# First attention of a two-layer decoder: row maxima and the stack of queries in chunks of 256 instead of 512

## The chip, the cores and the metric

The kernel runs on one core of one Trainium2 chip. TensorE (PE) multiplies matrices into PSUM banks, VectorE (DVE), ScalarE (ACT) and GpSimd (POOL) work beside it, and SyncE (SP) issues the DMAs. Each engine takes its own instructions strictly in the order in which the program gives them; semaphores order the engines among each other. The metric is the time of one execution on the device in microseconds (us). Before the change it was 2409.12 us, the median of 3 runs from 2406.58 to 2414.77 us.

## The reference, cut to what matters

Two decoder layers work on x of shape (4, 1024, 256). Each layer has a self-attention, a cross-attention to a short context, and a feed-forward part, all with a layer norm ahead and a residual behind. The change is in the first self-attention: 16 heads of 16 elements, causal, with a linear bias by distance (ALiBi).

```python
qkv = x @ w_attn.T                                   # x: 4 batches, 1024 tokens
att = jnp.einsum('bhqd,bhkd->bhqk', q, k) * (1.0 / math.sqrt(D))
bias = jnp.where(causal, slopes * rel, -jnp.inf)     # rel = key position - query position
att = jax.nn.softmax(att + bias[None], axis=-1)
y = jnp.einsum('bhqk,bhkd->bhqd', att, v)
```

The second layer's self-attention squares its scores instead of exponentiating them and has gates in place of the bias; the change touches it only in how queries are laid out.

## The kernel before

**Stages.** The first half of the execution does the first attention (`A0`) of batch 0, 1, 2, 3 in turn. Woven into batch b's attention are the cross-attention and feed-forward of batch b-1 and the preparation of weights. The second half does the same with the second attention (`A1`), from about 1274 us on, and ends with the last feed-forward.

**Groups and stacks.** `A0` takes the 16 heads in four groups of 4, so there are 16 groups over the four batches. For a group, `stacks` (L310) loads two tiles from DRAM on SP's queue. `QS` holds queries, `KS` keys, with 96 rows of split-up query and key parts (bf16, three parts each, in two sets of 48 rows), 12 rows for the bias, and two rows (108 and 109) for the negated row maximum of every query, split into a high and a low bf16 part. The product of a KS block with a QS block over all 110 rows is then the finished exponent: score plus bias minus row maximum. QS has shape [110, 2, 4, 512]: two halves of 512 queries, in each 4 heads. Its 96 rows are loaded with four DMAs (two sets of rows by two halves, L323), KS with two (L320), and one DMA each brings the bias rows (L325, L326). QS and KS have two buffers each. `A1` uses the same `stacks` for its 20 loads, without the bias rows.

**Row maxima.** `a0_max` (L339) goes through the scores once to find the maxima. One unit multiplies QS blocks of 128 queries with up to 512 keys into one PSUM bank (L352), adds the causal mask with a further matmul where the block lies on the diagonal (L356), and reduces with DVE (L357). The banks are named M and there are two (2 and 3), shared with the projections of queries, keys and values, named Q. A group has 38 units: 11 for the diagonal parts of queries 0 to 511, 11 for those of queries 512 to 1023, and 16 for the latter against keys 0 to 511. Then L372 joins the two sets of maxima of the second half.

**Putting them.** `a0_put_max` (L375) is called twice per group, after unit 11 and after unit 38. DVE negates 16 columns (L380), PE transposes them into an M bank (L381), ACT copies the high part (L383), DVE subtracts to get the low part (L384), and two DMAs on SP's queue write the rows 108 and 109 of one half of QS (L386).

**The main pass.** `a0_main` (L388) goes through the queries in four chunks c of 256 and through the key blocks j up to the diagonal: 2, 4, 6 and 8 units, 20 per group. A unit has four score matmuls (L401), with the mask (L403) where needed, two exponentials on ACT (L404), and, two units later, four products with the values (L413) into the one O bank. Chunks 0 and 1 read the first half of QS, chunks 2 and 3 the second.

**What sets the order.** `A0` (L470) weaves the main pass of group g with the loads and row maxima of group g+1, 20 main units to 25 or 38 units of the other side; in each batch the third group's side also holds the first 12 steps of the next batch's projections, and the fourth group's side the rest with the row maxima of that batch's first group. `schedule` weaves this with the side work. The result is only a priority. The framework then plans each engine's order with a time model of its own and takes later work ahead where it believes that earlier work is not ready. So the main pass of group g+1 begins in the measured order while the last maxima of group g+1 are still being made. That order is fixed when the program is built; it doesn't adapt on the chip.

Of the kernel before, what the change touches and what calls it, by code (L numbers as in the profile page):

```python
# [12 lines left out]
F32 = mybir.dt.float32  # L13
# [17 lines left out]
def const_arrays():  # L31
    bf = ml_dtypes.bfloat16
    c = {}
# [48 lines left out]
    c["alq"] = np.ascontiguousarray(rq.reshape(4, 4, 12, 2, 512).transpose(2, 0, 3, 1, 4)).astype(bf)  # L82
# [8 lines left out]
class Kern:  # L91
# [218 lines left out]
    def stacks(self, g, dr, alibi):  # L310

        nc = self.nc
        QS = self.t([110, 2, 4, 512], BF, "QS")
        KS = self.t([110, 4, T], BF, "KS")
        c, o = g // 2, (g % 2) * 4
        for st, t0 in ((QS, (1, 0)), (KS, (4, 5))):
            for r in range(2):
                v = dr[c][t0[r] : t0[r] + 3].rearrange("t (d h) n -> (t d) h n", h=8)[:, o : o + 4, :]
                if st is KS:
                    nc.sync.dma_start(KS[r * 48 : r * 48 + 48], v)  # L320
                else:
                    for a in range(2):
                        nc.sync.dma_start(QS[r * 48 : r * 48 + 48, a], v[:, :, a * 512 : a * 512 + 512])  # L323
# [15 lines left out]
    def a0_max(self, st, mt, tag="M"):  # L339
# [4 lines left out]
        def unit(pieces, diag, out):  # L344
# [6 lines left out]
            for x, (hh, i, k0, k1) in enumerate(pieces):  # L351
                nc.tensor.matmul(Sv[:, x, 0:w], QS[:108, i // 4, hh, i % 4 * 128 : i % 4 * 128 + 128], KS[:108, hh, k0:k1], start=x == 0, stop=not diag and x == n - 1)  # L352
# [6 lines left out]
        for part in range(2):  # L359
            b0 = part * 4  # L360
            yield unit([(hh, b0, part * 512, part * 512 + 128) for hh in range(4)], True, mt[:, :, b0])
            for p in range(2):
                yield unit([(p * 2 + e, b0 + 1, part * 512, part * 512 + 256) for e in range(2)], True, mt[:, p * 2 : p * 2 + 2, b0 + 1])
            for i in (2, 3):
                for hh in range(4):
                    yield unit([(hh, b0 + i, part * 512, part * 512 + (i + 1) * 128)], True, mt[:, hh, b0 + i : b0 + i + 1])
            if part == 0:
                self.a0_put_max(st, mt, 0)
        for i in range(4, 8):
            for hh in range(4):  # L370
                yield unit([(hh, i, 0, 512)], False, mt[:, hh, 4 + i : 5 + i])
        nc.vector.tensor_tensor(mt[:, :, 4:8], mt[:, :, 4:8], mt[:, :, 8:12], ALU.max)  # L372
        self.a0_put_max(st, mt, 1)

    def a0_put_max(self, st, mt, part):  # L375

        nc = self.nc
        ps = self.p("M")
        m8 = self.t([128, 4, 4], F32, "_m8")
        nc.vector.tensor_scalar(m8, mt[:, :, part * 4 : part * 4 + 4], -1.0, None, ALU.mult)  # L380
        nc.tensor.transpose(ps[:16, :128], m8.rearrange("p h i -> p (h i)"), self.ident)  # L381
        pr = self.t([16, 2, 128], BF, "VsJ")
        nc.scalar.activation(pr[:, 0, :], ps[:16, :128], AF.Copy)  # L383
        nc.vector.tensor_tensor(pr[:, 1, :], ps[:16, :128], pr[:, 0, :], ALU.subtract)  # L384
        for p in range(2):
            nc.sync.dma_start(st[0][108 + p : 109 + p, part].rearrange("o h (i n) -> o (h i) n", n=128), pr[:, p, :])  # L386

    def a0_main(self, st, V, y, g, O, pend):  # L388
# [3 lines left out]
        def scores(c, j):  # L392
# [4 lines left out]
            for p in range(2):  # L397
                S = self.p("S").rearrange("p (h k) -> p h k", h=2)
                for e in range(2):
                    hh = 2 * p + e  # L400
                    nc.tensor.matmul(S[:, e, 0:w], st[1][:110, hh, j * 128 : (j + 1) * 128], st[0][:110, q0 // 512, hh, q0 % 512 : q0 % 512 + w], start=e == 0, stop=not dg and e == 1)  # L401
# [421 lines left out]
    def A1(self, parts):  # L823
# [50 lines left out]
        def scores(r, b, g, c, j):  # L874
# [19 lines left out]
            for p in range(2):  # L894
                S = self.p("S").rearrange("p (h k) -> p h k", h=2)
                for e in range(2):
                    hh = 2 * p + e
                    nc.tensor.matmul(S[:, e, 0:w], st[r][1][:96, hh, j * 128 : (j + 1) * 128], st[r][0][:96, q0 // 512, hh, q0 % 512 : q0 % 512 + w], start=e == 0, stop=e == 1)  # L898
# [427 lines left out]
```

## Time and profile before

| What | Value |
|---|---|
| Median of 3 runs | 2409.12 us |
| The profiled execution | 2408.58 us |
| its span, from first to last instruction | 2406.8 us |
| PE busy | 2141.5 us (89%) |
| DVE busy | 1692.2 us (70%) |
| ACT busy | 1639.2 us (68%) |
| POOL busy | 1198.2 us (50%) |
| Reduces of the row maxima, L357 | 608, 386.2 us on DVE |
| Score matmuls for the maxima, L352 | 768, 225.8 us on PE |
| DMA | 238.45 MB, mean 99 GB/s |

The span is the time between the first and the last recorded instruction on the core; the execution's own time has 1.8 us around it. A busy time is the union of an engine's instructions. A row of the form "x608 | 386.2, 655 | 137.9 <-PE M L356 100.0" says: 608 instructions, 386.2 us busy together, 655 ns mean, 137.9 us in which the engine stood idle just before one of them, 100.0 us of that ended by the PE instruction of line 356. "PEclk" is the TensorE clock granted, as a share of full speed. L and a number is a line of the kernel before.

### The profile page before, as it was taken

To read this page: it belongs to the slowest core of one execution; us is meant where nothing else is said; L and a number is where in the kernel's file an instruction comes from. 1 tells how busy PE (TensorE), PEld (TensorE's weight loads), DVE (VectorE), ACT (ScalarE), POOL (GpSimd) and SP (SyncE) were. 2 spreads that over 40 slices of the span, in tenths; PEclk is the share of its full clock that TensorE was granted. 3 is DMA by queue.
4 is the path that set the end of the run, shared out by engine and by line. 5 is a ranking of instruction groups with operands and counts; after the bars stand their busy time and mean duration, and the time that the engine had idled before them with its cause. 6 is when DMAs were issued, how large, how long until landed. Compare 5 with 4: busy or idle time off the path is not lost.

```text
span 2406.8 us, 51445 instructions
## 1 busy us (share of the span) xinstructions
PE 2141.5 (89%) x19110; PEld 1510.9 (63%) x19110; DVE 1692.2 (70%) x3781; ACT 1639.2 (68%) x4173; POOL 1198.2 (50%) x1942
## 2 busy tenths in 40 slices
PE   6798899998999998899988988889988998899876
PEld 4454457755666654576656766567766766676675
DVE  4666657677766786776775677777867787777766
ACT  4365446676766676565778878987678777888542
POOL 7121313154331352412545458766867788775664
PEclk9899999999999999899989999999989999999988
DMA  8667331223841236231262224512241223542000
GB/s 260 199 193 211 116 90 44 66 61 108 242 135 44 64 111 188 69 73 41 81 185 53 71 71 129 149 38 56 98 111 43 56 74 119 105 98 71 10 10 18
DMA packets 182697, 238.45 MB, mean 99 GB/s; under 512 B 16198, under 2 KB 165846, under 8 KB 175958
## 3 DMA queue, kind: packets, MB, share of 16 engines
q1 hardware_dynamic: 182446, 235.15, 34.8%
q8 instruction: 151, 2.47, 0.4%
q14 instruction: 100, 0.82, 0.1%
HBM read 152.62 MB, written 82.21 MB: 98 GB/s over the span
## 4 chain that ended last, share of the span: by engine, by line
PE 59%; DVE 14%; DMA 8%; POOL 7%; ACT 7%; issue 3%; SPq 1%; POOLq 0%; DVEq 0%; ACTq 0%
PE T L191 10%; PE W L191 8%; PE O L413 7%; PE O L927 5%; PE S L401 5%; PE Q L191 4%; PE M L352 4%; PE S L898 3%; DVE P L904 2%; DVE s_mt L357 2%; PE W L630 1%; PE T L723 1%; DMA wst<-in_L_xattn_Wq 1%; POOL P L909 1%; ACT P L906 1%
## 5 line engine op out<-in xcount | busy, mean ns | idle before, releaser
L357 DVE TENSOR_REDUCE s_mt<-M 128x1 f32<-128x512 f32 (+3 forms) x608 | 386.2, 655 | 137.9 <-PE M L356 100.0
L404 ACT ACTIVATE P<-S 128x512 f32<-128x512 f32 (+1 forms) x640 | 342.4, 563 | 154.7 <-PE S L401 78.5
L906 ACT ACTIVATE P<-P,eps 128x1024 f32<-128x1024 f32 x320 | 344.5, 1082 | 57.2 <-DVE P L904 52.6
L904 DVE TENSOR_REDUCE P<-S 128x512 f32<-128x512 f32 (+1 forms) x480 | 284.8, 610 | 75.4 <-PE S L898 60.7
L352 PE MATMUL M<-KS,QS 108*128 108x512 bf16 (+3 forms) x768 | 225.8, 341 | 48.2 <-DVE s_mt L357 23.9
L191 PE MATMUL T<-R,xX 128*128 128x352 f32 (+1 forms) x1136 | 246.7, 331 | 4.8 <-ACT E L619 1.4
L898 PE MATMUL S<-QS,KS 96*128 96x256 bf16 (+1 forms) x1280 | 217.9, 269 | 36.9 <-DVE P L904 34.5
L401 PE MATMUL S<-QS,KS 110*128 110x256 bf16 (+1 forms) x1280 | 230.4, 267 | 16.9 <-ACT P L404 13.7
L413 PE MATMUL O<-P,V 128*32 128x256 f32 (+1 forms) x2560 | 240.1, 377 | 0.8 <-ACT P L404 0.6
L622 POOL TENSOR_TENSOR E<-E,s_xsm 128x616 f32<-128x616 f32 x64 | 77.9, 1217 | 323.7 <-DVE s_xsm L620 261.3
L191 PEld LDWEIGHTS T<-R,xX 128*128 128x128 f32 x1136 | 183.0, 190 | 24.7 <-ACT E L619 5.4
L191 PE MATMUL W<-R,xph 128*128 128x256 f32 (+1 forms) x952 | 185.4, 292 | 6.5 <-DVE xpl L180 4.8
L909 POOL TENSOR_TENSOR P<-P,y 128x512 f32<-128x512 f32 x128 | 165.1, 1299 | 34.0 <-ACT y L871 17.4
L619 ACT ACTIVATE E<-T,s_xmx 128x77 f32<-128x77 f32 x512 | 159.6, 334 | 28.6 <-DVE s_xmx L616 26.5
L401 PEld LDWEIGHTS <-KS 110*128 110x128 bf16 x1280 | 107.2, 100 | 105.6 <-issue 60.3
L927 PE MATMUL O<-P,VsJ 128*32 128x128 f32 x3584 | 168.2, 282 | 5.3 <-ACT P L906 4.8
L898 PEld LDWEIGHTS <-KS 96*128 96x128 bf16 x1280 | 101.8, 99 | 110.2 <-issue 88.9
L191 PEld LDWEIGHTS W<-R,xph 128*128 128x128 f32 (+1 forms) x952 | 149.5, 192 | 17.8 <-DVE xpl L180 6.9
L352 PEld LDWEIGHTS <-QS 108*128 108x128 bf16 x768 | 68.3, 100 | 128.0 <-issue 100.4
L191 PE MATMUL W<-R,xpl 128*128 128x256 f32 (+2 forms) x476 | 139.6, 293 | 1.0 <-DVE xpl L180 1.0
L730 POOL TENSOR_TENSOR R<-wst 128x256 f32<-128x256 f32 x128 | 92.3, 732 | 88.0 <-DVE wst L729 82.8
L179 ACT ACTIVATE xph<-W 128x512 fp32r<-128x512 f32 (+2 forms) x180 | 79.3, 458 | 80.1 <-PE W L633 32.8
(351 smaller groups left out, 5660.0 us busy)
## 6 DMA issues: line engine op xcount, KB each, us to landing
QS<-dr SPq DMA_DIRECT2D x144, 192.0 KB
KS<-dr SPq DMA_DIRECT2D x72, 384.0 KB
dr<-qp SPq DMA_DIRECT2D x32, 768.0 KB
MD<-R SPq DMA_DIRECT2D x24, 616.0 KB
UD<-R SPq DMA_DIRECT2D x24, 512.0 KB
R<-MD SPq DMA_DIRECT2D x32, 308.0 KB
X<-in_x SPq DMA_DIRECT2D x16, 512.0 KB
dr<-qp SPq DMA_DIRECT2D x32, 256.0 KB
```

Source lines behind the costliest of these rows:

```text
L191: nc.tensor.matmul(out, x, y, start=first and n == 0, stop=last and n == len(seq) - 1)
L352: nc.tensor.matmul(Sv[:, x, 0:w], QS[:108, i // 4, hh, i % 4 * 128 : i % 4 * 128 + 128], KS[:108, hh, k0:k1], start=x == 0, stop=not diag ...
L357: nc.vector.tensor_reduce(out, Sv[:, :, 0:w], AX.X, ALU.max)
L401: nc.tensor.matmul(S[:, e, 0:w], st[1][:110, hh, j * 128 : (j + 1) * 128], st[0][:110, q0 // 512, hh, q0 % 512 : q0 % 512 + w], start=e == ...
L404: nc.scalar.activation(P[:, 2 * p : 2 * p + 2, 256 - w :], S[:, :, 0:w], AF.Exp)
L413: nc.tensor.matmul(O[0][hh * 32 : hh * 32 + 32, o + o0 : o + 256], V[j // 4][:, j % 4, h * 17 : h * 17 + 32], P[:, hh, o0:], start=c % 2 = ...
L619: nc.scalar.activation(E[:, n * 77 : (n + 1) * 77], Sv[:, k, :], AF.Exp, bias=mx[:, n : n + 1], accum_out=sm[:, n : n + 1])
L898: nc.tensor.matmul(S[:, e, 0:w], st[r][1][:96, hh, j * 128 : (j + 1) * 128], st[r][0][:96, q0 // 512, hh, q0 % 512 : q0 % 512 + w], start= ...
L904: nc.vector.tensor_reduce(Pv, S[:, :, 0:w].unsqueeze(3), AX.X, ALU.max, apply_absolute_value=True)
L906: nc.scalar.activation(Pw, Pw, AF.Square, bias=self.eps1)
L909: nc.gpsimd.tensor_tensor(Pd, Pd, Ds[r, c][:, j - 2 * c], ALU.mult)
L927: nc.tensor.matmul(Oc[rows, o0 : o0 + 128], lhs, P[:, hh, c0 : c0 + 128], start=j == 2 * c and i == 2 * c, stop=fin and i == 2 * c + 1)
```

## The change

QS becomes [110, 4, 4, 256], four chunks of 256 queries, the chunks of the main pass. Its rows from DRAM come with eight DMAs of half the size instead of four, in runs of 512 bytes instead of 1024; the constant bias rows are laid out to match. The row maxima are made chunk by chunk, with 3, 8, 11 and 16 units (38 as before): for chunks 2 and 3 a block's diagonal units are followed at once by its units against keys 0 to 511. After each chunk its maxima are joined (chunks 2 and 3) and put, so there are four puts per group instead of two, each with 8 columns instead of 16. The main passes of both attentions address QS by chunk.

```diff
-    c["alq"] = np.ascontiguousarray(rq.reshape(4, 4, 12, 2, 512).transpose(2, 0, 3, 1, 4)).astype(bf)
+    c["alq"] = np.ascontiguousarray(rq.reshape(4, 4, 12, 4, 256).transpose(2, 0, 3, 1, 4)).astype(bf)
...
-        QS = self.t([110, 2, 4, 512], BF, "QS")
+        QS = self.t([110, 4, 4, 256], BF, "QS")
...
-                    for a in range(2):
-                        nc.sync.dma_start(QS[r * 48 : r * 48 + 48, a], v[:, :, a * 512 : a * 512 + 512])
+                    for a in range(4):
+                        nc.sync.dma_start(QS[r * 48 : r * 48 + 48, a], v[:, :, a * 256 : a * 256 + 256])
...
-                nc.tensor.matmul(Sv[:, x, 0:w], QS[:108, i // 4, hh, i % 4 * 128 : i % 4 * 128 + 128], KS[:108, hh, k0:k1], start=x == 0, stop=not diag and x == n - 1)
+                nc.tensor.matmul(Sv[:, x, 0:w], QS[:108, i // 2, hh, i % 2 * 128 : i % 2 * 128 + 128], KS[:108, hh, k0:k1], start=x == 0, stop=not diag and x == n - 1)
...
-        for part in range(2):
-            b0 = part * 4
-            yield unit([(hh, b0, part * 512, part * 512 + 128) for hh in range(4)], True, mt[:, :, b0])
-            for p in range(2):
-                yield unit([(p * 2 + e, b0 + 1, part * 512, part * 512 + 256) for e in range(2)], True, mt[:, p * 2 : p * 2 + 2, b0 + 1])
-            for i in (2, 3):
-                for hh in range(4):
-                    yield unit([(hh, b0 + i, part * 512, part * 512 + (i + 1) * 128)], True, mt[:, hh, b0 + i : b0 + i + 1])
-            if part == 0:
-                self.a0_put_max(st, mt, 0)
-        for i in range(4, 8):
-            for hh in range(4):
-                yield unit([(hh, i, 0, 512)], False, mt[:, hh, 4 + i : 5 + i])
-        nc.vector.tensor_tensor(mt[:, :, 4:8], mt[:, :, 4:8], mt[:, :, 8:12], ALU.max)
-        self.a0_put_max(st, mt, 1)
-
-    def a0_put_max(self, st, mt, part):
+        for c in range(4):
+            o = c // 2 * 512
+            for i in (2 * c, 2 * c + 1):
+                w = (i % 4 + 1) * 128
+                n = max(1, 512 // w) if w < 384 else 1
+                for h0 in range(0, 4, n):
+                    yield unit([(h0 + e, i, o, o + w) for e in range(n)], True, mt[:, h0 : h0 + n, i])
+                if c > 1:
+                    for hh in range(4):
+                        yield unit([(hh, i, 0, 512)], False, mt[:, hh, 4 + i : 5 + i])
+            t = slice(2 * c, 2 * c + 2)
+            if c > 1:
+                nc.vector.tensor_tensor(mt[:, :, t], mt[:, :, t], mt[:, :, 4 + 2 * c : 6 + 2 * c], ALU.max)
+            self.a0_put_max(st, mt[:, :, t], c)
+
+    def a0_put_max(self, st, mt, c):
...
-        m8 = self.t([128, 4, 4], F32, "_m8")
-        nc.vector.tensor_scalar(m8, mt[:, :, part * 4 : part * 4 + 4], -1.0, None, ALU.mult)
-        nc.tensor.transpose(ps[:16, :128], m8.rearrange("p h i -> p (h i)"), self.ident)
-        pr = self.t([16, 2, 128], BF, "VsJ")
-        nc.scalar.activation(pr[:, 0, :], ps[:16, :128], AF.Copy)
-        nc.vector.tensor_tensor(pr[:, 1, :], ps[:16, :128], pr[:, 0, :], ALU.subtract)
+        m8 = self.t([128, 4, 2], F32, "_m8")
+        nc.vector.tensor_scalar(m8, mt, -1.0, None, ALU.mult)
+        nc.tensor.transpose(ps[:8, :128], m8.rearrange("p h i -> p (h i)"), self.ident)
+        pr = self.t([8, 2, 128], BF, "VsJ")
+        nc.scalar.activation(pr[:, 0, :], ps[:8, :128], AF.Copy)
+        nc.vector.tensor_tensor(pr[:, 1, :], ps[:8, :128], pr[:, 0, :], ALU.subtract)
         for p in range(2):
-            nc.sync.dma_start(st[0][108 + p : 109 + p, part].rearrange("o h (i n) -> o (h i) n", n=128), pr[:, p, :])
+            nc.sync.dma_start(st[0][108 + p : 109 + p, c].rearrange("o h (i n) -> o (h i) n", n=128), pr[:, p, :])
...
-                    nc.tensor.matmul(S[:, e, 0:w], st[1][:110, hh, j * 128 : (j + 1) * 128], st[0][:110, q0 // 512, hh, q0 % 512 : q0 % 512 + w], start=e == 0, stop=not dg and e == 1)
+                    nc.tensor.matmul(S[:, e, 0:w], st[1][:110, hh, j * 128 : (j + 1) * 128], st[0][:110, c, hh, q0 - 256 * c : q0 - 256 * c + w], start=e == 0, stop=not dg and e == 1)
...
-                    nc.tensor.matmul(S[:, e, 0:w], st[r][1][:96, hh, j * 128 : (j + 1) * 128], st[r][0][:96, q0 // 512, hh, q0 % 512 : q0 % 512 + w], start=e == 0, stop=e == 1)
+                    nc.tensor.matmul(S[:, e, 0:w], st[r][1][:96, hh, j * 128 : (j + 1) * 128], st[r][0][:96, c, hh, q0 - 256 * c : q0 - 256 * c + w], start=e == 0, stop=e == 1)
```

## The prediction

> **What bounds the kernel now.** First the page: engines, and the PE and clock rows over the span.
>
> ```profile
> PE 2141.5 (89%) x19110; PEld 1510.9 (63%) x19110; DVE 1692.2 (70%) x3781; ACT 1639.2 (68%) x4173; POOL 1198.2 (50%) x1942
> PE   6798899998999998899988988889988998899876
> PEclk9899999999999999899989999999989999999988
> L357 DVE TENSOR_REDUCE s_mt<-M 128x1 f32<-128x512 f32 (+3 forms) x608 | 386.2, 655 | 137.9 <-PE M L356 100.0
> ```
>
> PE bounds the kernel; the first attention is the first 21 slices (1274 us). PE is not full there, so second, the timeline: where does the main pass stand still? Going through the first score matmul (L401) of each chunk, chunk 0 follows the previous group at once, but chunk 2 starts only 1.7 to 5.1 us after the issue of the second put's last DMA in 14 of 16 groups: it needs the second half's maxima. Third, the busy time in the 11 stretches from the end of chunk 1's score matmuls to the first of chunk 2 (the other five groups have none over 1.2 us); six of them:
>
> ```profile
> core 0: us, PE busy (x) PEld busy (x) DVE busy (x) ACT busy (x) POOL busy (x), PEclk, DMA share, GB/s
> 237.30:246.60 9.30, 6.46 (x37) 2.93 (x36) 6.64 (x13) 2.44 (x5) 0.00 (x0) 0.68 0.19 70
> 292.40:308.80 16.40, 12.17 (x49) 5.27 (x48) 9.88 (x19) 3.07 (x7) 4.99 (x6) 0.79 0.54 137
> 576.90:603.60 26.70, 21.39 (x120) 13.73 (x118) 18.21 (x41) 13.67 (x28) 12.98 (x15) 0.87 0.49 126
> 732.80:747.60 14.80, 14.11 (x105) 10.66 (x104) 11.51 (x27) 7.95 (x40) 2.00 (x2) 1.00 0.01 2
> 887.70:910.60 22.90, 17.86 (x95) 9.83 (x95) 17.06 (x40) 12.16 (x27) 9.49 (x13) 0.85 0.54 144
> 970.60:982.50 11.90, 8.24 (x50) 5.36 (x49) 11.65 (x26) 3.81 (x8) 4.63 (x5) 0.79 0.25 85
> sum 151.70, PE 125.09 PEld 81.26 DVE 109.77 ACT 70.86 POOL 43.35; mean PE 11.37 PEld 7.39 DVE 9.98 ACT 6.44 POOL 3.94
> ```
>
> The last row sums all eleven: 151.7 us, PE busy 125.1, so idle 26.6. Where other work is at hand (732.8) little is lost; where not, PE idles and the granted clock falls. The timeline of the second shows how:
>
> ```profile
> 296.10 0.38 PE L352 MATMUL M<-KS,QS 108*128 108x512 bf16 x1 [0.22 <-DVE s_mt L357]
> 296.70 0.38 PE L352 MATMUL M<-KS,QS 108*128 108x512 bf16 x1 [0.22 <-DVE s_mt L357]
> ...
> 303.96 0.41 PE L381 MATMUL M<-ident,s_m 128*16 128x128 f32 x1
> ...
> 308.84 0.39 PE L401 MATMUL S<-QS,KS 110*128 110x256 bf16 x2 [0.78 <-DMA QS<-VsJ]
> ```
>
> Maxima alone, at DVE's pace through two banks, then the put, then chunk 2 when the rows land.
>
> **Change, part by part.** *What goes.* Chunk 2 needs only its own put, after unit 22 of 38. The weave gives the maxima 25 units or more beside the 20 of the previous group's main pass, so unit 22 is before that pass ends. So its six units become free to fill the tail. A unit is four score matmuls and eight product records; those rows give 4 x 0.11 + 0.64, about 1.1 us of PE, 6.6 us for six, against at most 5.3 us idle in a stretch. The ceiling is 26.6 us of idle, and of the clock: the six stretches with a clock under 1 lack 1.7 (178.1 to 185.0, at 0.75), 3.0, 3.4, 3.5, 3.4 and 2.5 us of full clock, 17.5, times PE's share of 82%, 14.4. Ceiling 41; floor 0, if the planner places chunk 2 no earlier. The order is fixed by a plan that doesn't know the chip's times, so I take 60% of the idle (16) and half of the clock (7): gain 23.
>
> *What is late next.* Chunk 3 waits for the fourth put. From chunk 2's first to chunk 3's first score matmul passed 13.1 us (group from 308.84) to some 25 us. Sixteen reduces at 0.683 (10.9), join and negation (0.4), transpose to subtract (1.68 at the median) and landing (1.7 to 3.2) are 14.7 to 16.2. Even if they started only with chunk 2, the shortest case would be 3 us late.
>
> *Four puts.* 32 more in all. Durations by their rows:
>
> ```profile
> L381 PE MATMUL M<-ident,s_m 128*16 128x128 f32 x32 | 9.3, 289 | 2.2 <-DVE s_m L380 2.1
> L384 DVE TENSOR_TENSOR VsJ<-M,VsJ 16x128 bf16<-16x128 f32 x32 | 8.6, 269 | 7.3 <-ACT VsJ L383 7.1
> L383 ACT ACTIVATE VsJ<-M 16x128 bf16<-16x128 f32 x32 | 8.2, 258 | 15.9 <-PE M L381 15.9
> L380 DVE TENSOR_SCALAR s_m<-s_mt 128x16 f32<-128x16 f32 x32 | 7.7, 241 | 0.4
> ```
>
> PE: a transpose is between 0.11 (four pipelined, L430, took 0.60) and 0.29 us: 3.5 to 9.3, and 2.2 idle before it: 5.7 to 11.5. I take 7, near the pipelined end, as PE is mostly queued up. Behind a waiting transpose stand score matmuls and side work of all kinds.
> DVE: 32 x (0.241 + 0.269), 16 more joins of 0.20: 19.5, and 7.3 waiting for ACT, with reduces behind it. ACT: 8.2, and 15.9 waiting, with exponentials behind it. Both engines are under 71% and lie beside PE: nothing. Without that cover, 27 and 24.
> M bank: a put holds one of two for 1.68 us. If it costs what a unit costs PE (23.9 us before 608 reduces), 32 x 0.04 is 1.3; if PE waits out all that exceeds a reduce, 32 x 1.0 is 32. I take 2, as the woven order gives PE other banks' work.
> SP: 64 more issues at 0.55. SP stood 280 us at the 32 puts before (184.5 + 60.0 + 35.3); with twice the puts, loads of the side work, weights and next stacks stand behind them.
>
> ```profile
> SPq L386 <- ACT VsJ L383: 184.5, 16, 30.8
> PE M L352 <- DVE s_mt L357: 23.9, 49, 2.0
> ```
>
> Yet after its first 17 us PE hardly idled on such loads in this half (under 1 us by its waits), so I take 2. Ends: 0, and two mean stands (280/32 = 8.7) that reach PE, 17.
>
> *Eight query loads.* Each stack issues four more DMAs, 4 x 0.49 = 2.0 us on SP, ahead of the key loads, which are needed whole by the first unit. In the trace a packet of 1 KB took 46 ns and one of 512 bytes 27 ns at the median: 1536 x 27 - 768 x 46 over 16 engines is 0.4 us per stack. PE waited for a stack at groups 0 (4.3), 2 (2.2) and 3 (8.2, both put down to other transfers that came last), 7 (1.0) and 15 (4.4); elsewhere the first unit came 8 us or more after the last issue and didn't wait. So 5 x 0.4 to 5 x 2.0; I take 4. The second attention loads a run ahead, so its 20 stacks cost nothing; uncovered, 40.
> The bias rows, the unit order, the addressing: same counts and sizes, nothing either way.
>
> *Sum* against the profiled execution, 2408.6 (span 2406.8 and 1.8 around it; the median is 0.5 above): - 23 + 7 + 2 + 2 + 4 = -8, about 2400.
>
> Two rules of the Trainium skill speak otherwise, and the sum doesn't use them. "DMA: Bandwidth & Descriptors", section "Anatomy of one DMA", puts a fixed 2.0 us on each DMA of GpSimd's path. An estimate from it, were it paid in series on SP's path too, is 8 us per stack instead of 0.4 to 2.0, and so +32 instead of +4: 2428; the issues 0.44 us apart with shared landing speak against it. "TensorE: Matmul & The Clock Gate", section "HAM oscillation", has the clock fall after idle gaps over some 3.4 us. In the stretch from 292.4 no gap but one reaches 1 us and the clock is 0.79. By the rule the clock term is near 0 and the sum is 2408; by the row it stands.
>
> **Rivals.** *The wait moves (slower).* The plan, which believes the rows to be there, puts chunk 3 where chunk 2 was, right after the fourth put, and chunk 2 where it displaces side work that then is missing. Nothing is gained and 15 paid: 2424. For: PE is busy 93 to 98% in four of the eleven stretches (178.1, 414.9, 732.8 and 1050.4), so only the others can gain. Against: 13 us of cover and more. It decides where less than 15 of the 41 come back.
> *All comes back (faster).* Ceiling 41 less the low costs (5.7 + 1.3 + 0 + 2.0 = 9.0): -32, 2377. For: 6.6 us of chunk 2 exceed every stretch's idle. Against: three of the waits (308.8, 603.6, 910.6) fall into the projections of the next batch, which compete for the M banks.
> *Nothing new.* The planner already takes work ahead and does much the same: costs and gains cancel, 2409.
> *Puts stall the queues.* Bank and SP at their upper ends (32 and 17) with the gain kept: -23 + 7 + 32 + 17 + 4, +37: 2446.
>
> **How the numbers follow.** 0.3% (7.2 us) is about what a measurement can tell from no change. Forecast (2392 to 2410 for gains of 13 to 31): 0.40, of which 0.25 is beyond 7.2 us faster. All comes back: 0.19. Nothing new: 0.08. The wait moves (2414 to 2432): 0.25. Stalled queues: 0.08. Faster 0.25 + 0.19 = 0.44; same 0.15 + 0.08 = 0.23; slower 0.33. The range leaves out the better half of "all comes back" and most of the stalled queues, 0.17: 2383 to 2434.
>
> **What would show it.** Right: the sums of idle between chunk 1 and chunk 2 fall from 26.6 to near 10, chunk 2 starts well before the fourth put, granted clock near 1 in those stretches; 64 transposes (L381's successor) at under 0.3 us with some 5 us idle before them; 288 query loads. Wrong: a new idle of the same size before chunk 3; idle before L352 on DVE rising by more than 10 us; key loads landing over 2 us later after the first issue; PE waiting for side loads behind puts.

## The result and the profile after

The changed kernel takes 2523.59 us (median of 4 runs, 2519.41 to 2528.64) against 2411.94 us before in the same comparison: 1.0447 times as long, 95% interval 1.0416 to 1.0478. The forecast was 2400, the range 2383 to 2434. The profiled execution took 2522.78 us with a span of 2521.0.

By stage (the first attention lasts until the last score matmul of its main pass ends):

| | before, us | after, us |
|---|---|---|
| first attention ends at | 1273.7 | 1373.1 |
| of it PE busy / idle | 1150.8 / 122.9 | 1227.5 / 145.6 |
| second attention | 986.3 | 993.3 |
| after it | 146.8 | 154.6 |

So 99 us are lost in the first attention, 77 of them as more PE work and 23 as idle time, and 15 us behind it. The page of after, the lines that answer to those of before:

```profile
PE 2234.8 (89%) x19108; PEld 1539.3 (61%) x19142; DVE 1724.5 (68%) x3861; ACT 1648.9 (65%) x4205; POOL 1200.4 (48%) x1942
PE   5898999998989999799988998799988998899876
PEclk9799999999999999899998999999999999999988
L357 DVE TENSOR_REDUCE s_mt<-M 128x1 f32<-128x512 f32 (+3 forms) x608 | 388.6, 656 | 176.7 <-PE M L356 116.6
L412 PE MATMUL O<-P,V 128*32 128x256 f32 (+1 forms) x2560 | 295.3, 374 | 3.8 <-ACT P L403 3.7
L352 PE MATMUL M<-KS,QS 108*128 108x512 bf16 (+3 forms) x768 | 226.8, 341 | 40.8 <-DVE s_mt L357 29.4
L400 PE MATMUL S<-QS,KS 110*128 110x256 bf16 (+1 forms) x1280 | 230.0, 269 | 25.0 <-DMA QS<-VsJ 12.8
```

From `a0_max`'s end on, lines stand one lower than before (L412 was L413, L400 was L401). The work that the change adds does not show here. What shows is an operation that it does not touch: the value products. The same group of before, from its page:

```profile
L413 PE MATMUL O<-P,V 128*32 128x256 f32 (+1 forms) x2560 | 240.1, 377 | 0.8 <-ACT P L404 0.6
```

The same 2560 records of nearly the same mean duration cover 55 us more. The timeline says why: first before, then after (start and duration in us; the `S` row behind a burst shows when PE is through with it).

```profile
455.11 0.64 PE L413 MATMUL O<-P,V 128*32 128x256 f32 x8
455.69 0.39 PE L401 MATMUL S<-QS,KS 110*128 110x256 bf16 x2
```

```profile
454.51 0.38 PE L400 MATMUL S<-QS,KS 110*128 110x256 bf16 x2
454.82 0.63 PE L412 MATMUL O<-P,V 128*32 128x256 f32 x4
455.38 0.39 PE L400 MATMUL S<-QS,KS 110*128 110x256 bf16 x2
455.70 0.62 PE L412 MATMUL O<-P,V 128*32 128x256 f32 x4
456.26 0.66 PE L629 MATMUL W<-ident,E 128*128 128x128 f32 x4
```

The four products of a unit are eight records, one pair for each of the four heads, and each head has its own 32 columns of the array. Together they occupy PE for 0.58 us up to the next start. If PE takes the first two heads as soon as their exponential is there and the other two later, each half occupies it for 0.56 us. At the median over the trace it is 0.57 us for eight records, 0.56 for four and 0.55 for two. The Trainium skill, "TensorEngine Tiling (Array Packing)", section "Tiling Modes", says that tiles in different columns can work in parallel; these rows agree. Before, the products of the first attention stood in 395 uninterrupted bursts (245 of eight records), after in 493 (149 of eight, 307 of four). 98 bursts more times 0.56 would be 55 us. That is a little too much, as not all bursts are that long: where the products have 128 columns instead of 256, a burst holds PE for 0.34 to 0.36 us, again whether it has two, four or eight records. Summed over all bursts, the time from a burst's first record to the next other start grows from 220.0 to 265.3 us, by 45 us.

Second, the stretches ahead of the chunks, from the end of one chunk's score matmuls to the first of the next, for every one of over 1.2 us. The sum rows for the stretches ahead of chunk 1, 2 and 3, with two of those ahead of chunk 2:

```profile
sum 84.90, PE 68.86 PEld 42.12 DVE 68.78 ACT 46.70 POOL 27.55; mean PE 4.92 PEld 3.01 DVE 4.91 ACT 3.34 POOL 1.97
...
234.80:247.00 12.20, 4.96 (x31) 1.50 (x29) 8.01 (x13) 1.26 (x4) 0.00 (x0) 0.74 0.88 268
442.50:451.00 8.50, 8.03 (x59) 5.70 (x58) 6.64 (x17) 4.29 (x21) 1.06 (x1) 1.00 0.01 2
...
sum 108.30, PE 81.26 PEld 47.80 DVE 75.49 ACT 50.04 POOL 30.91; mean PE 5.80 PEld 3.41 DVE 5.39 ACT 3.57 POOL 2.21
...
sum 90.20, PE 81.66 PEld 57.83 DVE 52.69 ACT 39.02 POOL 23.02; mean PE 5.83 PEld 4.13 DVE 3.76 ACT 2.79 POOL 1.64
```

Ahead of chunk 2 PE is idle for 108.3 - 81.3 = 27.0 us, where it was 26.6. Ahead of chunk 1 it is 16.0 (4.7 before), ahead of chunk 3 it is 8.5 (none before). Ahead of each of the chunks 1, 2 and 3 there are now 14 such stretches (5, 11 and 5 before), and 32 of the 64 chunks start within 6 us of the issue of their own put's last DMA. Chunk 2 does start before the fourth put in 15 of 16 groups (at 451.0 us in the sixth, where the fourth put's DMAs are issued from 474.2 us on), as foretold, and nothing is won by it: the fourth put comes later, and chunk 2 no sooner. The sixth group, from the last score matmul of the group ahead of it to the put that chunk 2 needs and to chunk 2's first score matmul; first before, then after:

```profile
392.39 0.28 PE L401 MATMUL S<-QS,KS 110*128 110x128 bf16 x2
...
423.90 0.27 PE L381 MATMUL M<-ident,s_m 128*16 128x128 f32 x1
...
428.40 0.61 PE L401 MATMUL S<-QS,KS 110*128 110x256 bf16 x4 [0.41 <-DMA QS<-VsJ]
```

```profile
416.12 0.28 PE L400 MATMUL S<-QS,KS 110*128 110x128 bf16 x2
...
447.42 0.27 PE L380 MATMUL M<-ident,s_m 128*8 128x128 f32 x1
...
451.04 0.61 PE L400 MATMUL S<-QS,KS 110*128 110x256 bf16 x4
```

The put after unit 38 came 31 us after the end of the previous group's pass, and now the put after unit 22 comes there. On the mean of 15 groups (the first has none ahead of it) chunk 2 started 34.8 us after that end, and now starts 34.2 us after it. The maxima have fallen behind instead: the put after unit 11 came 14.9 us ahead of that end and now comes 3.7 us behind it, the put after unit 38 came 28.5 us behind it and now comes 51.1 us behind it.

### The profile page after: what moved, and what is told of

It reads as the page before. It is cut to its first block, busy times and chain, and to the rows that moved or that the text cites. A ratio compares the mean times of both kernels' runs of the same rounds, so it can differ in the third digit from the quotient of the medians.

```text
span 2521.0 us, 51899 instructions
## 1 busy us (share of the span) xinstructions
PE 2234.8 (89%) x19108; PEld 1539.3 (61%) x19142; DVE 1724.5 (68%) x3861; ACT 1648.9 (65%) x4205; POOL 1200.4 (48%) x1942
## 4 chain that ended last, share of the span: by engine, by line
PE 61%; DVE 15%; POOL 7%; DMA 7%; ACT 6%; issue 3%; SPq 1%; POOLq 0%; DVEq 0%; ACTq 0%
PE T L191 10%; PE O L412 9%; PE W L191 8%; PE O L926 5%; PE S L400 5%; PE Q L191 4%; PE M L352 4%; PE S L897 3%; DVE P L903 2%; DVE s_mt L357 2%; DMA QS<-VsJ 2%; PE W L629 1%; DMA wst<-in_L_xattn_Wq 1%; PE T L722 1%; PE S L402 1%
## 5 line engine op out<-in xcount | busy, mean ns | idle before, releaser
L357 DVE TENSOR_REDUCE s_mt<-M 128x1 f32<-128x512 f32 (+3 forms) x608 | 388.6, 656 | 176.7 <-PE M L356 116.6
L412 PE MATMUL O<-P,V 128*32 128x256 f32 (+1 forms) x2560 | 295.3, 374 | 3.8 <-ACT P L403 3.7
L352 PE MATMUL M<-KS,QS 108*128 108x512 bf16 (+3 forms) x768 | 226.8, 341 | 40.8 <-DVE s_mt L357 29.4
L400 PE MATMUL S<-QS,KS 110*128 110x256 bf16 (+1 forms) x1280 | 230.0, 269 | 25.0 <-DMA QS<-VsJ 12.8
L400 PEld LDWEIGHTS <-KS 110*128 110x128 bf16 x1280 | 104.8, 100 | 121.2 <-issue 65.4
L352 PEld LDWEIGHTS <-QS 108*128 108x128 bf16 x768 | 69.4, 100 | 119.1 <-issue 99.8
L412 PEld LDWEIGHTS O<-P,V 128*32 128x32 f32 x2560 | 74.1, 108 | 108.0 <-issue 98.7
```

The lines of the kernel that those rows point to most:

```text
L352: nc.tensor.matmul(Sv[:, x, 0:w], QS[:108, i // 2, hh, i % 2 * 128 : i % 2 * 128 + 128], KS[:108, hh, k0:k1], start=x == 0, stop=not diag ...
L357: nc.vector.tensor_reduce(out, Sv[:, :, 0:w], AX.X, ALU.max)
L412: nc.tensor.matmul(O[0][hh * 32 : hh * 32 + 32, o + o0 : o + 256], V[j // 4][:, j % 4, h * 17 : h * 17 + 32], P[:, hh, o0:], start=c % 2 = ...
```

## The experiments

All times are medians; ratios are to runs of the kernel before on the same chip, with their 95% interval. "First" is the end of the first attention in the profiled execution, "rest" what follows it, both in us; "bursts" are the uninterrupted stretches of value products, and idle is PE's in the first attention.

| run | us | ratio | first | rest | bursts | idle |
|---|---|---|---|---|---|---|
| before | 2411.94 | 1 | 1273.7 | 1133.1 | 395 | 122.9 |
| layout and eight loads only | 2428.62 | 1.0068 [1.0044, 1.0092] | 1276.0 | 1155.2 | 392 | 121.5 |
| four puts, old layout | 2506.96 | 1.0402 [1.0367, 1.0436] | 1355.3 | 1148.3 | 503 | 132.1 |
| unit order only | 2440.67 | 1.0125 [1.0091, 1.0159] | 1288.6 | 1154.5 | 397 | 126.4 |
| puts for 0+1, 2, 3 | 2498.58 | 1.0358 [1.033, 1.0386] | 1363.9 | 1140.6 | 470 | 147.8 |
| puts for 0, 1, 2+3 | 2434.25 | 1.0093 [1.0062, 1.0124] | 1303.7 | 1132.3 | 395 | 136.4 |
| puts for 0+1+2, 3 | 2429.63 | 1.0069 [1.004, 1.0099] | 1293.9 | 1136.1 | 412 | 128.6 |
| after, products whole | 2467.04 | 1.0225 [1.0203, 1.0248] | 1318.7 | 1146.5 | 342 | 167.3 |
| before, products whole | 2431.61 | 1.0067 [1.0047, 1.0087] | 1281.1 | 1150.9 | 345 | 140.7 |
| after, transposes in T | 2506.29 | 1.0391 [1.0354, 1.0427] | 1357.1 | 1148.2 | 442 | 156.7 |
| after, transposes in S | 2463.11 | 1.0211 [1.0183, 1.0238] | 1311.1 | 1147.9 | 425 | 128.1 |
| the same, products whole | 2446.20 | 1.0145 [1.0114, 1.0176] | 1294.7 | 1150.6 | 341 | 152.8 |
| unit order, 32 spare puts | 2475.21 | 1.0263 [1.0231, 1.0296] | 1329.9 | 1141.9 | 387 | 157.1 |
| unit order, 64 spare puts | 2476.50 | 1.0275 [1.0248, 1.0301] | 1336.1 | 1136.8 | 389 | 156.5 |
| 64, without their DMAs | 2526.99 | 1.0484 [1.0453, 1.0516] | 1384.7 | 1143.2 | 413 | 175.4 |
| 64, DVE's part only | 2449.68 | 1.0151 [1.0118, 1.0184] | 1299.3 | 1152.6 | 393 | 141.8 |
| 64, transposes in S | 2490.91 | 1.0325 [1.0297, 1.0354] | 1335.2 | 1154.9 | 420 | 142.7 |
| before, keys first | 2412.46 | 1.0009 [0.9992, 1.0027] | 1257.5 | 1153.6 | 378 | 116.7 |
| before, own bank for puts | 2503.45 | 1.0380 [1.0347, 1.0413] | 1349.5 | 1151.3 | 372 | 178.6 |
| after | 2523.59 | 1.0447 [1.0416, 1.0478] | 1373.1 | 1147.9 | 493 | 145.6 |

**Each part alone.** *The layout and the eight loads*, with the unit order and the two puts of before:

```diff
-        QS = self.t([110, 2, 4, 512], BF, "QS")
+        QS = self.t([110, 4, 4, 256], BF, "QS")
...
-                    for a in range(2):
-                        nc.sync.dma_start(QS[r * 48 : r * 48 + 48, a], v[:, :, a * 512 : a * 512 + 512])
+                    for a in range(4):
+                        nc.sync.dma_start(QS[r * 48 : r * 48 + 48, a], v[:, :, a * 256 : a * 256 + 256])
```

> The chunked layout of QS and its eight loads of 512-byte runs, with the unit order and the two puts per group of before (each put writes two chunks). Theory A (the four puts lengthen the pass of the maxima through its two banks and change the order): near before, 2400 to 2425 us, with about 395 bursts of value products as before. Theory B (the loads are late, or the order is planned for slower loads): most of the 112 us is here, 2490 us or more, with maxima that start 45 to 55 us after the first query load as in the changed kernel (before: about 30).

*The chunk order and four puts on the old layout*, with four DMAs per put instead of two, as a chunk is not one run of a row there:

```diff
+            self.a0_put_max(st, mt[:, :, t], c)
...
+            for i in range(2):
+                k = c % 2 * 256 + i * 128
+                nc.sync.dma_start(st[0][108 + p : 109 + p, c // 2, :, k : k + 128], pr[i * 4 : i * 4 + 4, p, :])
```

> The unit order and the four puts per group of the change, with the layout and the four query loads of before; since a chunk is not contiguous in that layout, each put needs four DMAs instead of two. Theory A: slow as the changed kernel, 2500 to 2540 us, about 500 bursts of value products, pass of the maxima 8 us longer per group. Theory B: near before, 2405 to 2430 us.

*The unit order alone*, two puts, old layout:

```diff
-            self.a0_put_max(st, mt[:, :, t], c)
+            if c == 3:
+                nc.vector.tensor_tensor(mt[:, :, 4:8], mt[:, :, 4:8], mt[:, :, 8:12], ALU.max)
+            if c % 2:
+                self.a0_put_max(st, mt, c // 2)
```

> Only the order of the units by chunk, with two puts per group, layout and loads of before. Theory A: near before, 2400 to 2430 us. Theory C (the order of the units, diagonal and full ones alternating, is what slows the maxima): 2480 us or more.

The first and the third lie 4 and 11 us above the band that was expected for them, by less than they lose in the rest. The layout moves the end of the first attention by 2.3 us, the unit order by 15; the four puts bring nearly the whole of the loss, with 503 bursts. All three also lose 15 to 22 us in the rest. That is not their own work: in the run with the unit order the first 5450 PE instructions of the rest stand in the same sequence as before and take 585.6 us against 584.5; where the sequences part, what follows takes 20 us more. The build plans the whole program anew for every edit, and the plan of before is a good draw: over all versions the rest is 1132 to 1155 us. The loss in the first attention is no such accident of one plan, as four versions that put chunk 2 by itself, with three or four puts in the banks M or T, lie together: the changed kernel, the one with four puts on the old layout, and two that follow, at 2499 to 2524 us.

**Which release does it?** Versions of the changed kernel with fewer puts, each for several chunks:

```diff
+PUTS = {1: (0, 2), 2: (2, 1), 3: (3, 1)}     # or {0: (0, 1), 1: (1, 1), 3: (2, 2)} or {2: (0, 3), 3: (3, 1)}
...
-            self.a0_put_max(st, mt[:, :, t], c)
+            if c in PUTS:
+                self.a0_put_max(st, mt, *PUTS[c])
```

> Chunked layout as in the change, three puts per group: chunks 0 and 1 together, chunk 2, chunk 3. Theory D (the release of chunk 2 ahead of chunk 3 reorders the work: the main pass runs beside its own maxima, the next group's maxima come later, and the value products of a unit are issued in two half bursts): most of the loss, 2470 to 2515 us, some 470 bursts. Theory E (every extra put costs the same by itself): half of the loss, about 2465, and the same as the next run.

> Chunked layout, three puts per group: chunk 0, chunk 1, chunks 2 and 3 together. As many puts as the run before it. Theory D: close to the run with layout and loads alone, 2410 to 2445 us, some 395 bursts. Theory E: about 2465 us.

> Two puts per group as in the kernel before, with the layout of four chunks and eight query loads: the first put covers chunks 0, 1 and 2 together (after unit 22), the second chunk 3 alone. The number of puts, of transposes and of put DMAs is that of the kernel before. Theory 'early release of chunk 2' (the loss comes from chunk 2's main pass being let go ahead of the maxima of chunk 3, so that it runs beside them in half bursts and the pass of the maxima gets longer): clearly slower than the version with the unit order alone (2440.67), at least +15 us, so 2455 to 2500; value products in more than 410 bursts; waits of PE for a put's landing well above that version's 6.0 us. Theory 'number of puts' (the loss comes from four transposes, evictions and pairs of DMAs per group instead of two): within 15 us of 2440, so 2425 to 2455, near 397 bursts.

With equally many puts, those for 0+1, 2 and 3 lose 87 us and those for 0, 1 and 2+3 lose 22. That looked like chunk 2's early release, but the third version releases it as early and loses 17: the theory of the early release, which wanted 2455 or more, falls in that form. Its trace is the most telling one of the study. Chunk 2 no longer waits at all, and the idle time ahead of it is 3.9 us where the unit order alone has 39.5. Ahead of chunk 0 it is 55.9 instead of 5.4; the stretches of that kind, two of them and the sum:

```profile
213.90:228.40 14.50, 5.90 (x38) 2.72 (x37) 8.31 (x18) 2.44 (x6) 4.31 (x4) 0.70 0.98 216
...
955.90:981.90 26.00, 11.37 (x64) 5.08 (x63) 18.84 (x40) 4.88 (x11) 7.80 (x10) 0.65 0.94 232
...
sum 236.30, PE 180.52 PEld 113.73 DVE 184.83 ACT 115.78 POOL 63.55; mean PE 13.89 PEld 8.75 DVE 14.22 ACT 8.91 POOL 4.89
```

PE's idle time in the first attention is 128.6 us, against 126.4. The row of the stretches ahead of chunk 2 in that run:

```profile
sum 13.40, PE 9.48 PEld 6.06 DVE 6.38 ACT 6.61 POOL 2.57; mean PE 1.90 PEld 1.21 DVE 1.28 ACT 1.32 POOL 0.51
```

The idle time moved and did not shrink. The stretch in which the maxima run with little beside them lies ahead of whichever chunk the main pass stops at.

**What do half bursts cost?** One GpSimd multiplication by 1 of the last column of a unit's exponentials makes its products wait for both of them:

```diff
+            nc.gpsimd.tensor_scalar(P[:, :, 255:256], P[:, :, 255:256], 1.0, 1.0, ALU.mult, ALU.mult)
             return P, 256 - w
```

> The changed kernel with one more instruction per main unit: GpSimd multiplies the last column of the four heads' exponentials by 1, so that no value product can start before both exponentials are done and all eight records stand together. 320 such instructions of 4 columns, on an engine that is half idle. If half bursts are what costs (a burst of four records takes 0.56 us, one of eight 0.57): bursts fall from 493 to about 340, 150 x 0.56 = 84 us less, 2430 to 2460 us. If half bursts only fill time in which PE waits for the maxima anyway: 2500 us or more.

> The same instruction in the kernel before. If half bursts cost as much as whole ones: bursts fall from 395 to about 345, 50 x 0.56 = 28 us less, 2375 to 2395 us. If not: 2405 to 2430 us.

In the changed kernel the bursts fall from 493 to 342 and the time by 56.6 us, less than the 84 that 0.56 us for each burst would give, and that in spite of 22 us more idle time. PE's busy time in the first attention falls by 76 us, most of it in the products. In the kernel before the bursts fall by 50, PE's busy time by 10 us, and its idle time rises by 18: the run is 20 us slower, 7 of them in the first attention. The products of the changed kernel, held whole, on its page:

```profile
L413 PE MATMUL O<-P,V 128*32 128x256 f32 (+1 forms) x2560 | 212.1, 379 | 7.3 <-POOL P L404 6.0
```

They cover 212.1 us of PE instead of 295.3. The split products are thus about half of the loss. With the products whole on both sides the change costs 35 us (2467.04 against 2431.61) instead of 112. Both runs have a plan of their own, so these are sizes and not exact prices.

**The bank of the puts' transposes.** Two variants, T (the side work's three banks) and S (the main pass's two) instead of M:

```diff
-        ps = self.p("M")
+        ps = self.p("T")     # or self.p("S")
```

> The changed kernel with the transposes of the puts in the three banks T instead of the two banks M. Theory A1 (what the four puts cost is the M bank that each holds): at least half of the loss comes back, 2440 to 2470 us or less; reduces on both sides of a put no further apart than others. Theory A2 (the puts' hops between the engines cost by themselves, or the early release of the chunks does): 2500 us or more.

> The changed kernel with its put transposes in the two score banks (S) of the main pass instead of the two of the maxima (M), nothing else. In the program's order its value products stand in 425 bursts instead of 493, and 0 to 4 main units of a group instead of 11 to 14 stand ahead of the next group's first maximum. Theory 'split value products': 68 bursts fewer at 0.56 us, 38 us faster than the changed kernel's 2523.59, so about 2485. Theory 'order of the two passes' (the loss comes from the next group's maxima starting late): clearly more, 2440 to 2470. Theory 'M bank': likewise below 2485, with PE's idle time ended by a reduce of the maxima back at the level of the kernel before. If only the extra puts' work counts: no change, 2510 to 2530.

In T the transpose queues behind side work. It comes 31.8 us after its chunk's last reduce on the mean (2.6 after the change as made), and the run says nothing on the bank itself. In S the loss falls from 112 to 51 us. 68 bursts fewer would be 38 us of it at 0.56; the products cover 30 us less on the page (265.5 against 295.3). PE's idle time in the first attention falls by 18 us, to 128.1. That this comes from the other order of the two passes, and not from the bank itself, is argued from the trace. No chunk starts within 6 us of its put any more (32 did), as the main pass of a group now starts at about its third or fourth put (438.1 us in the sixth, with puts at 381.3, 391.7, 430.1 and 439.0), and PE's weight loads wait 1.8 us for landings instead of 17.1. The maxima's matmuls (L352) and the products on that page:

```profile
L352 PE MATMUL M<-KS,QS 108*128 108x512 bf16 (+3 forms) x768 | 222.3, 341 | 48.7 <-DMA KS<-c_alk 17.3
L412 PE MATMUL O<-P,V 128*32 128x256 f32 (+1 forms) x2560 | 265.5, 377 | 0.2
```

The put that chunk 2 needs now comes 7.8 us ahead of the end of the previous group's pass on the mean, where it came 24.3 us behind it, and yet chunk 2 starts 31.2 us behind that end instead of 34.2. So it is not the put alone that holds chunk 2 back, but also the work that the plan places ahead of it. PE's idle time ahead of L352 that a reduce ended is 15.7 us, where the changed kernel has 29.4. With the products held whole in addition:

> The same with, in addition, one GpSimd multiply by 1 of the last column of a unit's exponentials (320 in all), so that the value products of a unit wait for both exponentials and stay whole: 341 bursts in the program. Theory 'split value products': 84 bursts fewer at 0.56 us, 47 us faster than the run without it, less 7 to 18 us for the longer wait as it cost in the kernel before. If the two effects add up, this is the changed kernel's best form: some 30 to 40 us below the run beside it and below the 2467 of the whole products alone, near 2445. It is not expected to be faster than the kernel before.

2446.2, close to what was expected, but 17 us from the extra edit instead of 29 to 40: PE is busy 41 us less and idle 25 us more. This is the best form of the change, and it is still 1.45% slower than the kernel before.

**What does a put cost?** The unit order with its two puts, and spare puts that release nothing: negated, transposed, evicted and sent to a scratch buffer that nobody reads.

```diff
+            if c % 2 == 0:                       # the 64: after every chunk
+                self.a0_spare_put(mt, c)
             if c == 3:
...
+        nc.vector.tensor_scalar(m8, mx, -1.0, None, ALU.mult)
+        nc.tensor.transpose(ps[:8, :128], m8.rearrange("p h i -> p (h i)"), self.ident)
+        pr = self.t([8, 2, 128], BF, "VsJ")
+        nc.scalar.activation(pr[:, 0, :], ps[:8, :128], AF.Copy)
+        nc.vector.tensor_tensor(pr[:, 1, :], ps[:8, :128], pr[:, 0, :], ALU.subtract)
...
+        for p in range(2):
+            nc.sync.dma_start(d[p], pr[:, p, :])
```

> Chunk order and two releases per group as in the version with the unit order alone, plus two spare puts per group: after chunks 0 and 2 their maxima are negated, transposed, evicted and sent by two DMAs each to a scratch buffer that nobody reads. The output does not change. It is the work of the two extra puts without what they release. Theory 'early release': 2440.67 plus only the extra work, 32 transposes with their 5.8 us of PE time and up to as much again for their bank, so 2440 to 2458; bursts 380 to 410. Theory 'number of puts': most of the 112 us come back, above 2480.

34.5 us over the unit order alone, between the two theories' numbers. In the first attention it is 41 us, 1.3 us per spare put, and almost all of it lies in the stretches ahead of chunk 2, where the maxima run alone: their sum row has 290.1 - 213.2 = 76.9 us of idle time, against 176.0 - 136.5 = 39.5 in the run with the unit order alone (second).

```profile
sum 290.10, PE 213.21 PEld 141.53 DVE 197.94 ACT 117.03 POOL 75.47; mean PE 14.21 PEld 9.44 DVE 13.20 ACT 7.80 POOL 5.03
```

```profile
sum 176.00, PE 136.47 PEld 88.83 DVE 125.30 ACT 74.76 POOL 42.84; mean PE 10.50 PEld 6.83 DVE 9.64 ACT 5.75 POOL 3.30
```

To tell the parts of a put apart the spare puts were doubled, and parts left out:

> Base for all four runs: the version with the unit order alone, whose first attention ended at 1288.6 us (2440.67 in all). Two spare puts per group into a scratch buffer nobody reads moved that end by 41.3 us (32 puts, 1.3 us each), where the prediction had 11 for the transposes, the bank and SP's queue. Here a spare put follows every chunk, 64 in all, so that its parts can be told apart in the next runs. If the price is one of the puts and not of a newly drawn order, it doubles: the first attention ends near 1371 (1350 to 1390). If it was the draw: 1310 to 1345.

> The 64 spare puts without their 128 DMAs: join, negation, transpose, ACT's copy and DVE's subtraction stay. Theory 'SP's queue' (loads of the side work stand behind the put's DMAs): the first attention ends 30 us or more before the run with the DMAs, below 1330. Theories 'M bank' and 'chain on DVE': within 15 us of the run with the DMAs.

> Of the 64 spare puts only DVE's work: join, negation and a subtraction of the same columns from SBUF, some 0.5 us per put on DVE; no transpose, no bank, no work on ACT, no DMA. Theory 'chain on DVE' (the pass of the maxima goes at DVE's pace, and whatever DVE does between two reduces is paid): 64 times 0.5, the first attention ends 25 to 40 us after 1288.6, near 1320. Theory 'M bank' or 'SP's queue': within 12 us of 1288.6.

> The 64 spare puts with their transposes in the two banks of the main pass's scores (S) instead of the two of the maxima (M). Theory 'M bank' (the put holds one of the two banks through which matmul and reduce alternate): most of the price goes, the first attention ends at least 40 us before the run with M, near 1300 to 1330, and PE's idle time ended by a reduce falls back to the base's. Theory 'chain on DVE' or 'SP's queue': within 15 us of the run with M.

The price does not double: 48 us for 64 against 41 for 32. The end at 1336.1 us lies in the band that was set for a newly drawn order (1310 to 1345), not in that of a price for each put. DVE's part costs 11. Without its DMAs the same work costs 96 us, twice as much as with them. Moving the transposes to S takes away the idle time by reduces (46.8 us ahead of L352 in the page with M, 19.6 with S) but gives it back in 31 more bursts, and the end does not move (1335.2 against 1336.1), where the theory of the M bank wanted at least 40 us. So transposes and evictions seem to cost something that DVE's part and the DMAs do not explain, but two plans for nearly the same work lie up to 49 us apart here, and no closer price for a single put can be read from such runs. This stays open.

**Is there something to take in the kernel before?** The key loads ahead of the query loads in `stacks`, and a bank of their own for the puts (the side work's T then has two banks instead of three):

```diff
-        for st, t0 in ((QS, (1, 0)), (KS, (4, 5))):
+        for st, t0 in ((KS, (4, 5)), (QS, (1, 0))):
```

> The kernel before with the key loads of a group issued ahead of its query loads, nothing else. Theory 'every edit of the planned order draws again' (the planner orders the work of the whole kernel anew, and the second half varies by -2 to +29 us between versions that do not touch it): within 2395 to 2445, most likely slower by 0.3 to 1%. If fewer split bursts alone decided, the 378 bursts that this order has in the program would give 395 - 378 = 17 bursts times 0.56 us, 9 us faster: 2402.

```diff
-        "O": (7,), "T": (4, 5, 6), "W": (4, 5, 6)},
+        "O": (7,), "T": (4, 5), "W": (4, 5), "MP": (6,)},
...
-        ps = self.p("M")
+        ps = self.p("MP")
```

> The kernel before with a PSUM bank of its own for the transpose of the puts (bank 6, which leaves the side work's T banks two instead of three), nothing else. If fewer split bursts decide, its 372 bursts in the program give 23 times 0.56 us, 13 us faster: 2399. If the draw of the order and the side work's missing bank decide: 2405 to 2450, side work later in the first attention, its tail longer. Tells whether the kernel before, with its two releases, leaves something that a small edit can take.

The first wins 16 us in the first attention and loses 20 in the rest, which it does not touch: no change. The second, though it has 23 bursts fewer, is 3.8% slower, outside both expectations: 56 us more idle in the first attention. The side work's missing third bank is the likely reason, but the order is another one too, and the run does not part the two. No version was faster than the kernel before.

## Why the prediction was wrong

*The bound.* PE does bound the first attention, 90% busy before and 89% after. The reading that its stretches ahead of chunk 2 are where time can be had was wrong. So was "chunk 0 follows the previous group at once" for one group: the eighth starts 20.5 us after the seventh ends (534.3 to 554.8 us), though PE is idle for only 3.2 of them.

*What goes: -23.* This step failed. The 26.6 us of idle time were counted as recoverable, 60% of them. They became 27.0, with 11 more ahead of chunk 1 and 8.5 ahead of chunk 3. The premise that failed is "unit 22 is before that pass ends": in the changed kernel the put after unit 22 comes 11 to 48 us after the end of the previous group's pass in all 15 groups that have one, 24.3 on the mean. Chunk 2 starts 34.2 us after that end, where it was 34.8. That is the floor of 0 that the step itself names ("if the planner places chunk 2 no earlier") and to which the sum gave no weight. The version with puts for 0+1+2 and 3 shows that even where the idle time does vanish ahead of chunk 2 (to 3.9 us), it comes up elsewhere and the end does not come earlier. In the kernel before, that stretch was also the time in which the maxima got ahead at their best pace, 0.60 us a unit, with nothing beside them; that this is what kept the products whole later is argued from the traces, not shown by a run. The clock's share of the gain (7) did not come either: half clock in the first attention went from 105.8 to 126.3 us.

*A missing term.* Split value products were in no step and no rival. The prediction took a unit as 1.1 us of PE wherever it is placed, with 0.64 for its products; with the products in halves it is 4 x 0.11 + 1.12, about 1.6. It put this at nothing without a reason, and it is the largest single term: 45 us of PE by the bursts of the two traces, 56.6 us of time by the run that holds the products together.

*What is late next: covered.* Chunk 3 does wait now, for 8.5 us of idle time in 14 stretches, about a third of the 23 us by which idle grew. The estimate that 13 us of cover suffice left out that chunk 2 now runs beside chunk 3's maxima, which take longer there. Sixteen reduces up to the landing were to take 14.7 to 16.2 us; from the third put's transpose to the fourth's alone pass 26.8 us on the mean. The 38 units of a group's maxima take 71 us from first to last reduce on the mean, 65.5 before.

*Four puts.* The transposes by themselves were right, 64 of them at 282 ns with 3.8 us of idle time ahead:

```profile
L380 PE MATMUL M<-ident,s_m 128*8 128x128 f32 x64 | 18.1, 282 | 3.8 <-DVE s_m L379 2.5 <-DVE yTl L180 1.0
```

PE's time in them that nothing overlaps grew by 5.8 us, where 7 was taken. DVE's part at nothing was near: 11 us for twice as many. The sum of the puts at 11 was probably too low, as 32 spare puts cost 41 us and 64 cost 48, but plans for nearly the same work differ by as much. Whether the bank at 2 us was wrong stays open. Moving the put transposes out of M gives 60 of the 112 us back, with another order of the passes; moving those of the 64 spare puts gives 1. SP's queue at 2 us was not the trouble: taking away the DMAs of the spare puts brought no gain.

*Eight query loads: 4.* Right in size: 2.3 us in the first attention of one execution each, which is hardly to be told from nothing. The estimate of +32 that was weighed beside it, in series from the 2.0 us for each DMA of GpSimd's path (the Trainium skill, "DMA: Bandwidth & Descriptors", section "Anatomy of one DMA"), does not come out here. It also took four stacks of 8 us, where the sum counted five. The 20 stacks of the second attention cost nothing by themselves that could be told apart from the 20 us by which the plans of the rest differ, and this spread was a bound that the sum lacked.

*The rivals.* "The wait moves" named the right place and got its condition (less than 15 of the 41 came back) but not the size: 15 us instead of 112. "Puts stall the queues" at +37 came nearest in number only: no run shows its bank term, and its term for SP did not show. Of the signs, two spoke: idle ahead of chunk 2 unchanged and a new one, a third of its size, ahead of chunk 3. A third misled: chunk 2 starts well before the fourth put, which was to show the prediction right. The one that was named for the bank, idle ahead of L352 ended by the reduces, rose by only 5.5 us; what rose was DVE's idle time ahead of its reduces (L357), by 39 us.

*How much is explained.* Holding the products whole (57 us alone) and moving the transposes to S with the order that this brings (60 alone) overlap: both together give 77 us. Of the 35 that remain, 21 are in the first attention, of the size of the unit order's 15, and the rest in the second half, whose plans vary by that much. Why the planner places the main pass behind each put when the transposes are in M, and far behind when they are in S, was not shown.

## What to carry to other kernels

Idle time ahead of a wait is not a gain until it is known what else that stretch does: look at PE's total idle time of the stage, and expect that an earlier release moves the gap. Before a wait is counted as a gain, check in the trace that the work which it holds back could start sooner at all. Operations that share PE by column groups were only cheap side by side here; count their uninterrupted bursts before and after any edit that lets them start earlier. Where a planner orders the whole program, an edit of one stage redraws all others; here that alone moved untouched code by up to 22 us, and nearly equal work by up to 49, so a forecast needs that spread in its range.

## What was not expected of the hardware

- A burst of two heads' value products holds PE as long as one of four heads (0.56 us against 0.57), and one of one head nearly so (0.55). With 128 columns instead of 256 all three hold it for 0.34 to 0.36 us.
- With two PSUM banks instead of three for the side work (and the third for the puts) the first attention took 76 us longer, in the one version that tried it, whose order was planned anew as well.
- Holding the products of 320 units back behind a GpSimd instruction of 209 to 218 ns each added 18 and 22 us to PE's idle time. In the first attention it cost 7 us in the kernel before and won 54 in the changed one.
